# A two-layer residual kernel: the second product of odd units cut in two around the first, and low-rank banks copied out by the scalar engine

## The chip, the cores and the metric

The kernel runs on one core of a Trainium2 chip. TensorE (PE) multiplies, VectorE (DVE) adds and subtracts, ScalarE (ACT) copies, GpSimd (POOL) and SyncE (SP) issue transfers. The metric is device time in microseconds, the median of three runs; a profile of one execution shows where it goes.

## The reference

All data are fp32. `x` has 32 sequences of 128 rows and 2048 columns. Two layers are added one after the other:

```python
x = x + (einsum('bsi,oi->bso', x, W0) + bias
         + scale[id0][:, None, None] * einsum('bsr,bor->bso', einsum('bsi,bri->bsr', x, A[id0]), B[id0]))
x = x + einsum('bij,bkj->bik', x, W1[id1])      # W1: 16 matrices of 2048x2048, one chosen per sequence
```

`W0` is one 2048x2048 matrix for all sequences. `A` and `B` are low-rank adapters of rank 16, chosen per sequence.

## The kernel before, in words

**Two stages.** Stage one computes the first layer for all sequences, stage two the second layer, pair of sequences by pair of sequences. Both replace multiplications by sums: a block product is done with seven products in place of eight. In stage one this is done twice over: seven *phases* (`PHASES`) on the outside, and in each of them seven products P1 to P7 inside a unit. `PHASES[i]` says which blocks of `x` (A terms) and of `W0` (W terms) DVE has to add up, which partial result the unit reads and writes, and whether it finishes a quarter of the output (`final`).

**Units.** Stage one is a list of 56 units: 7 phases x 2 groups of sequences x 4 column blocks, in that order, so a group change comes every four units. Phases 3 to 6 (units 24 to 55) are final. Of these, units 24 to 31 also write a new partial result; the code calls them `apart`. In units 32 to 55 the even ones are `late` and the odd ones `ahead`.

**Accumulators.** The eight PSUM banks are pairs a, b and c (one of each for even and for odd units) and the two banks d and l. A product of four matmuls (`product`, L500) puts 128x512 results into one bank. The order in a unit, on PE, is P1 into a; P2 into b; P6 onto a; P5 into c; P7 onto a; P3 onto c; P4 onto a. So P6 can't start before ACT has copied P1's result out of bank a into `p1` (L619). ACT likewise copies `u2` (L648) after P6, `p5` (L651) after P5, `u3` (L656) after P7, and the last quarter (L687) after P4. DVE adds the pairs b+p1, c+u2 and u3+p5 into quarters of the result `z`.

**The low-rank part.** `add_low` (L511) multiplies the low-rank factors of a unit, four short matmuls for each of four banks. In an `apart` unit it runs at the unit's start, into b, c, d and l; DVE then adds each of the four banks to a tile of `x` (`low_to_x`), and the products reuse b and c. In a `late` (even) unit it runs at the unit's end, for the unit itself onto b, c, a and into d, and for the odd unit that follows into that unit's b, c, a and bank l. Of the odd unit's four, b stays where it is, and P2 is accumulated onto it, which is why P2 comes before P1 there:

```python
            if ahead:
                product(2, b, n, False)
            if n != 1:
                product(1, a, n, True)
                nc.scalar.copy(p1, a)
                if not ahead:
                    product(2, b, n, True)
```

The other three banks (a1, c1 and l in the code) are read out by DVE in `low_to_x`, the first of them ahead of three adds of the even unit's own quarters.

**What sets the order.** The order of instructions on every engine is the order of the text; nothing is scheduled by a planner. An engine waits at an instruction until the semaphores that the framework derived from its operands are reached. `finish(n-1)`, called at the start of unit n, adds partial results and `x` to `z` and stores it by POOL. `w_terms`, `w_sums`, `a_terms` and `a_sums` are the DVE sums for units and groups to come. Loads are begun by `Loads.pump` on SP's queue, in a fixed list, as soon as a slot of `mem` is free; slots are freed as DVE and PE finish with them. `evp` holds one buffer for each of p1, u2, p5 and u3.

**Unit 0** also does P1 and P2 of unit 1, and keeps the copy of P1 in a tile of its own, `p1_next`.

**Stage two** (L728) has 7168 recorded matmuls of 128x512 into the same eight banks, on weights that SP loads two steps ahead.

Of the kernel before, what the change touches and what calls it, by code (L numbers as in the profile page):

```python
# [9 lines left out]
F32 = mybir.dt.float32  # L10
# [62 lines left out]
def cond_resid_kernel(  # L73
# [56 lines left out]
    nc = tc.nc  # L130
    B, S, D = out.shape
    NW, _, _, _, P, _, _, NF = w1q.shape
# [44 lines left out]
    def add(dst, a, b):  # L177
        nc.vector.tensor_tensor(dst, a, b, ALU.add)  # L178
# [83 lines left out]
    with tc.tile_pool(name="c0", bufs=1) as c0, tc.tile_pool(  # L262
        name="ev", bufs=1
# [17 lines left out]
        def view(slot, *shape):  # L281
            names = "abcd"[: len(shape)]
            return mem[:, slot].rearrange(
                f"p ({' '.join(names)}) -> p {' '.join(names)}", **dict(zip(names[1:], shape[1:]))
            )
# [39 lines left out]
        def early(n):  # L325

            return n < len(units) and PHASES[units[n][0]][4] and (
                PHASES[units[n][0]][3] or n % 2 == 1
            )
# [58 lines left out]
        def make_scale():  # L388

            id0_f = c0.tile([P, B // 4], F32, tag="id0f", name="id0_f")  # L390
            nc.vector.tensor_scalar(id0_f, id0r_sb, 0.0, float(NA - 1), ALU.max, ALU.min)
            hit = c0.tile([P, B // 4], F32, tag="hit", name="hit")
            for n in range(NA):
                nc.vector.tensor_scalar(
                    hit if n else scale, id0_f, float(n), scl[:, n : n + 1],
                    ALU.is_equal, ALU.mult,
                )
                if n:
                    add(scale, scale, hit)
# [85 lines left out]
        def load_b(n):  # L485
            i, g, o = units[n]
            r, c, _ = PHASES[i][4]
            b_sel = bsp.tile([P, 4, P], F32, tag="b_sel", name="b_sel")
            for t in range(2):
                for s in range(4):  # L490
                    m = adapter(id0_ok, 16 * r + 8 * g + 4 * t + s, NA - 1, POOL)
                    nc.gpsimd.dma_start(  # L492
                        out=b_sel[ts(t, 2 * RT), s],
                        in_=bt[ds(m, 1), c, o].rearrange("o j r m -> (o j r) m"),
                    )
            return b_sel

        def product(k, dst, n, start):
            for i in range(4):
                nc.tensor.matmul(  # L500
                    dst, lhsT=wts[n][k][:, i, :], rhs=acts[n // 4][k][:, i, :],
                    start=(start and i == 0), stop=(i == 3), skip_group_check=True,
                )

        def add_low(n, dsts, starts):

            i, g, o = units[n]
            r = PHASES[i][4][0]
            for s in range(4):
                for q, (dst, start) in enumerate(zip(dsts, starts)):  # L510
                    nc.tensor.matmul(  # L511
                        dst[:, ts(s, S)], lhsT=b_sels[n][ts(q, RT), s], rhs=low[r, g][ts(q, RT), s],
                        start=(start and s == 0), stop=(s == 3), skip_group_check=True,
                    )
# [2 lines left out]

            return z.rearrange("p (t s j m) -> p t s j m", t=2, s=4, j=2)[:, t, :, j]

        def low_to_x(n, q, src):  # L520
            xs = view(loads.slot(("x", n)), 4, NF)[:, q]
            add(xs, src, xs)

# [57 lines left out]
        for n, (i, g, o) in enumerate(units):  # L581
            _, _, old, new, final = PHASES[i]
            a, b, c = (x[n % 2] for x in (bank_a, bank_b, bank_c))
            z = mem[:, 19 + n % 2]
            group = n // 4
            more = group + 1 < 2 * len(PHASES)
            lowering = more and (group + 1) // 2 == LOW
            apart = bool(new and final)
            late = final and not early(n)
            ahead = early(n) and not apart  # L590
            p1, u2, p5, u3 = (
                evp.tile([P, NF], F32, tag=k, name=k) for k in ("p1", "u2", "p5", "u3")
            )
            if n == 1:
                p1 = p1_next
            if n + 1 < len(units) and PHASES[units[n + 1][0]][4]:
                b_sels[n + 1] = load_b(n + 1)
            if apart:
                low_banks = b, c, bank_d, bank_l
                add_low(n, low_banks, (True,) * 4)  # L600
                for q in range(4):
                    low_to_x(n, q, low_banks[q])
            if n:
                finish(n - 1)
            if n == 2:
                make_scale()
            if n == len(units) - 2:
                load_w1(0)
            if 0 < n < len(units) - 1:
                wts[n + 1] = w_sums(n + 1)  # L610
            elif n:
                second_loads()
            sums = a_sums(group + 1) if more and o == 3 else iter(())

            if ahead:
                product(2, b, n, False)
            if n != 1:
                product(1, a, n, True)
                nc.scalar.copy(p1, a)  # L619
                if not ahead:  # L620
                    product(2, b, n, True)
            if n == 0:
                p1_next = c0.tile([P, NF], F32, tag="p1_next", name="p1_next")
                product(1, bank_a[1], 1, True)
                nc.scalar.copy(p1_next, bank_a[1])
                product(2, bank_b[1], 1, True)
            if lowering:
                lowrank(group + 1, o)
                loads.done(("a", group + 1, o))
            if more:  # L630
                a_terms(group + 1, o)
            if n + 2 < len(units):
                w_terms(n + 2)
            if lowering and o % 2 == 1:
                lowrank_out(group + 1, o // 2)
            ends = n + 1 == len(units)
            if ends:
                rest = mem[:, loads.slot(("U4", n))]
                for t in range(2):
                    dst = rest.rearrange("p (t s j m) -> p t j s m", t=2, s=4, j=2)[:, t]  # L640
                    add(dst, dst, view(loads.slot(("x", n)), 2, 2, 4, S)[:, t])
                loads.done(("x", n))
            if not late:
                add(zq(z, 0, 0), by_seq(b), by_seq(p1))
            if ends:
                add(zq(z, 0, 0), zq(z, 0, 0), zq(rest, 0, 0))
            product(6, a, n, False)
            nc.scalar.copy(u2, a)  # L648
            next(sums, None)
            product(5, c, n, True)  # L650
            nc.scalar.copy(p5, c)  # L651
            if ends:
                fourth = sums_w1(0)
            next(sums, None)
            product(7, a, n, False)
            nc.scalar.copy(u3, a)  # L656
            add(zq(z, 1, 1), by_seq(u3), by_seq(p5))
            if ends:
                add(zq(z, 1, 1), zq(z, 1, 1), zq(rest, 1, 1))
                sums_x1(0, 0)  # L660
            next(sums, None)
            product(3, c, n, False)
            if not late:
                add(zq(z, 0, 1), by_seq(c), by_seq(u2))
            if ends:
                add(zq(z, 0, 1), zq(z, 0, 1), zq(rest, 0, 1))
                store_x1(n, 0)
            product(4, a, n, False)
            next(sums, None)
            if late:  # L670
                add_low(n, (b, c, a, bank_d), (False, False, False, True))

                b1, c1, a1 = (x[1 - n % 2] for x in (bank_b, bank_c, bank_a))
                add_low(n + 1, (b1, c1, a1, bank_l), (True,) * 4)
                low_to_x(n + 1, 2, a1)
                add(zq(z, 0, 0), by_seq(b), by_seq(p1))
                add(zq(z, 0, 1), by_seq(c), by_seq(u2))
                add(zq(z, 1, 1), by_seq(bank_d), zq(z, 1, 1))
                low_to_x(n + 1, 1, c1)
                low_to_x(n + 1, 3, bank_l)  # L680
            if ends:
                add(zq(z, 1, 0), by_seq(a), zq(rest, 1, 0))
                store_x1(n, 1)
                loads.done(("U4", n))
                fourth()
            else:
                nc.scalar.copy(zq(z, 1, 0), by_seq(a))  # L687
            loads.done(("W", n, 0))
            if o == 3:
                for q in range(4):  # L690
                    loads.done(("A", group, q, 0))


    with tc.tile_pool(name="c1", bufs=1) as c1:
# [6 lines left out]
        for n in range(last + 1):  # L701
# [22 lines left out]
            for k in (1, 6, 7, 5, 2, 3, 4) if n == last else (1, 7, 2, 3, 5, 6, 4):  # L724
                dst = bank[:, banks[k]]
# [108 lines left out]
```

## Time and profile before

| | |
|---|---|
| median of three runs | 2988.7 us (2988.65 to 2988.78) |
| the profiled execution | 2988.26 us, span 2986.6 us |
| PE busy | 2964.9 us (99%) |
| DVE busy | 2351.8 us (79%) |
| ACT busy | 183.6 us (6%) |
| POOL busy | 239.0 us (8%) |
| mean transfer rate | 343 GB/s |
| stage one ends | about 1443.5 us |

The span is the time from the first to the last instruction of the profile; the execution's own time is 1.66 us more. In the profile's rows "p" stands for p1 and p5, "u" for u2 and u3, since buffer numbers are left out, and "mem", "bank" and "tset" are the big tiles. L178 and L181 are the one-line helpers `add` and `sub` through which all DVE adds and subtractions go, so their rows hold many uses. One fp32 matmul of the code leaves two records, and two weight loads. The time behind a row in square brackets is that for which the engine stood idle before it, and what ended that.

### The profile page before, as it was taken

Reading aid. Unit: us, or ns where it says so; the run is one execution under the profiler, and the core shown is the slowest. Engines: PE = TensorE matmul, PEld = TensorE weight load, DVE = VectorE, ACT = ScalarE, POOL = GpSimd, SP = SyncE. Lnnn points to the kernel's source line nnn. Section 1 sums busy time; section 2 is a strip of 40 time slices with the busy share of each in tenths; the row PEclk is TensorE's granted clock in tenths of the full one; section 3 lists DMA queues with packets and bytes.
Section 4 is the critical chain, followed back from the end, with each engine's and each line's share of the span. In section 5 each row is a group of like instructions: output and inputs, shape, how many; then the busy total and the mean of one; then the engine's idle time right before and its main releaser. Section 6 shows DMA issues by size and latency. Waiting matters only on the chain.

```text
span 2986.6 us, 32858 instructions
## 1 busy us (share of the span) xinstructions
PE 2964.9 (99%) x12384; PEld 1171.9 (39%) x12384; DVE 2351.8 (79%) x1717; ACT 183.6 (6%) x312; POOL 239.0 (8%) x427
## 2 busy tenths in 40 slices
PE   9999999999999999999999999999999999999999
PEld 4445444444444444444333333333333333333333
DVE  3467755467645768873999999999999999999997
ACT  1111111111111111111000000000000000000000
POOL 1111000022212222221000000000000000000000
PEclk9999999999999999999999999999999999999999
DMA  5679866789865889986899999999999999999995
GB/s 225 257 307 368 322 258 268 270 302 345 323 259 208 312 340 374 380 319 261 335 399 392 387 387 410 385 400 386 405 387 398 386 388 405 392 395 386 403 391 220
DMA packets 186014, 1025.61 MB, mean 343 GB/s; under 512 B 23808, under 2 KB 23808, under 8 KB 79616
## 3 DMA queue, kind: packets, MB, share of 16 engines
q1 hardware_dynamic: 142512, 906.68, 76.7%
q0 software_dynamic: 25248, 83.92, 7.4%
q10 hardware_dynamic: 18096, 32.91, 3.5%
q8 instruction: 98, 1.61, 0.2%
q14 instruction: 60, 0.49, 0.0%
HBM read 922.76 MB, written 100.66 MB: 343 GB/s over the span
## 4 chain that ended last, share of the span: by engine, by line
PE 74%; DVE 1%; DMA 0%; ACT 0%; issue 0%; ACTq 0%; DVEq 0%
PE bank L728 52%; PE bank L500 22%; PE bank L511 1%; DMA mem<-in_w0q_dram 0%; DVE mem L178 0%; ACT p L619 0%; DVE mem L181 0%; DVE tset L181 0%; DVE res L178 0%; ACTq L619 0%; DVEq L178 0%; DVEq L181 0%
## 5 line engine op out<-in xcount | busy, mean ns | idle before, releaser
L181 DVE TENSOR_TENSOR mem<-mem 128x2048 f32<-128x2048 f32 (+1 forms) x733 | 1483.1, 2052 | 42.5 <-DMA mem<-in_w0q_dram 16.0
L728 PE MATMUL bank<-mem 128*64 128x512 f32 x5120 | 1120.6, 592 | 0.0
L500 PE MATMUL bank<-mem 128*128 128x512 f32 x1792 | 792.7, 595 | 6.2 <-DVE mem L178 4.7
L728 PEld LDWEIGHTS bank<-mem 128*64 128x64 f32 x5120 | 367.7, 137 | 731.1 <-issue 695.2
L500 PE MATMUL bank<-mem,tset 128*128 128x512 f32 x1344 | 597.1, 594 | 9.2 <-ACT p L619 9.2
L500 PEld LDWEIGHTS bank<-mem 128*128 128x128 f32 x1792 | 339.6, 191 | 429.5 <-issue 421.4
L728 PE MATMUL bank<-mem,s 128*64 128x512 f32 x2048 | 461.2, 592 | 0.0
L178 DVE TENSOR_TENSOR mem<-mem 128x2048 f32<-128x2048 f32 (+2 forms) x195 | 338.8, 1750 | 101.8 <-ACT mem L687 51.4
L500 PEld LDWEIGHTS bank<-mem,tset 128*128 128x128 f32 x1344 | 253.5, 190 | 333.3 <-issue 309.2
L728 PEld LDWEIGHTS bank<-mem,s 128*64 128x64 f32 x2048 | 147.1, 137 | 292.4 <-issue 291.5
L178 DVE TENSOR_TENSOR mem<-u,p 128x512 f32<-128x512 f32 x56 | 38.7, 691 | 213.8 <-ACT u L656 213.8
L492 POOL DMA_DIRECT2D b_sel<-in_bt_dram x256 | 134.7, 526 | 349.7 <-PE bank L511 186.5
L178 DVE TENSOR_TENSOR mem<-bank,mem 128x512 f32<-128x512 f32 x81 | 51.4, 684 | 104.4 <-PE bank L511 104.4
L734 ACT COPY pv<-bank 128x512 f32<-128x512 f32 x32 | 18.8, 586 | 1516.1 <-PE bank L728 1136.2
L178 DVE TENSOR_TENSOR pv<-bank,pv 128x512 f32<-128x512 f32 x64 | 44.3, 692 | 78.4 <-PE bank L728 77.4
L181 DVE TENSOR_TENSOR tset<-mem,tset 128x512 f32<-128x512 f32 x112 | 77.2, 689 | 7.9 <-PE bank L500 4.1
L178 DVE TENSOR_TENSOR mem<-bank,u 128x512 f32<-128x512 f32 x56 | 38.5, 688 | 53.8 <-PE bank L500 53.8
L178 DVE TENSOR_TENSOR mem<-mem,ident 128x1024 f32<-128x1024 f32 x64 | 78.1, 1220 | 0.0
L530 POOL DMA_DIRECT2D x1t<-mem x64 | 49.0, 770 | 224.3 <-DVE mem L178 220.4
L648 ACT COPY u<-bank 128x512 f32<-128x512 f32 x56 | 32.8, 586 | 356.9 <-PE bank L500 353.1
L687 ACT COPY mem<-bank 128x512 f32<-128x512 f32 x55 | 32.2, 586 | 356.2 <-PE bank L500 242.9
L619 ACT COPY p<-bank 128x512 f32<-128x512 f32 x55 | 32.2, 586 | 231.1 <-PE bank L500 224.8
(40 smaller groups left out, 507.9 us busy)
## 6 DMA issues: line engine op xcount, KB each, us to landing
mem<-in_w1q_dram SPq DMA_DIRECT2D x512, 1024.0 KB, 10.2
mem<-in_xq_dram SPq DMA_DIRECT2D x119, 1024.0 KB, 12.6
mem<-in_w0q_dram SPq DMA_DIRECT2D x111, 1024.0 KB, 6.8
mem<-U SPq DMA_DIRECT2D x40, 1024.0 KB, 9.4
mem<-in_xq_dram SPq DMA_DIRECT2D x66, 512.0 KB, 7.9
x1t<-mem POOLq DMA_DIRECT2D x64, 512.0 KB, 8.9
mem<-x1t SPq DMA_DIRECT2D x64, 512.0 KB, 10.0
out_dram<-res ACTq DMA_DIRECT2D x124, 256.0 KB, 6.1
```

The costliest lines, as they stand in the source:

```text
L178: nc.vector.tensor_tensor(dst, a, b, ALU.add)
L181: nc.vector.tensor_tensor(dst, a, b, ALU.subtract)
L492: nc.gpsimd.dma_start(out=b_sel[ts(t, 2 * RT), s], in_=bt[ds(m, 1), c, o].rearrange("o j r m -> (o j r) m"),)
L500: nc.tensor.matmul(dst, lhsT=wts[n][k][:, i, :], rhs=acts[n // 4][k][:, i, :], start=(start and i == 0), stop=(i == 3), skip_group_check=True,
L511: nc.tensor.matmul(dst[:, ts(s, S)], lhsT=b_sels[n][ts(q, RT), s], rhs=low[r, g][ts(q, RT), s], start=(start and s == 0), stop=(s == 3), s ...
L530: nc.gpsimd.dma_start(out=x1t[4 * r + 2 * g + t][:, :, 8 * c + 2 * o : 8 * c + 2 * o + 2].rearrange("s p j m -> p s (j m)"), in_=view(19 + ...
L619: nc.scalar.copy(p1, a)
L648: nc.scalar.copy(u2, a)
L687: nc.scalar.copy(zq(z, 1, 0), by_seq(a))
L728: nc.tensor.matmul(dst[ts(j, M)], lhsT=xts[pair, k4 // 2][k][:, j, k4 % 2 * 2 + i], rhs=w1s[n][k][:, j, i], start=(k4 == 0 and i == 0), st ...
L734: nc.scalar.copy(pv[:, 0], dst)
```

## The change

`product` takes the list of its matmuls as an argument. In `ahead` units only the first two matmuls of P2 come before P1, and the other two come after P1 and its copy. A tile `kept` of two banks' size is added; `p1_next` becomes its first half. `low_to_x` can have ACT copy the bank into `kept` first, and DVE then adds from `kept`: this is done for banks b and c of the `apart` units (q = 0 and 1) and for bank a1 of the odd unit in `late` units, where the copy comes in ACT's order ahead of the copy of the last quarter (L687). DVE's adds and their order stay, as do the number and order of all loads and stores.

```diff
-        def product(k, dst, n, start):
-            for i in range(4):
+        def product(k, dst, n, start, some=range(4)):
+            for i in some:
...
+        kept = c0.tile([P, 2, NF], F32, tag="kept", name="kept")
+
-        def low_to_x(n, q, src):
+        def low_to_x(n, q, src, k=None):
+            if k is not None:
+                nc.scalar.copy(kept[:, k], src)
+                src = kept[:, k]
             xs = view(loads.slot(("x", n)), 4, NF)[:, q]
             add(xs, src, xs)
...
                 for q in range(4):
-                    low_to_x(n, q, low_banks[q])
+                    low_to_x(n, q, low_banks[q], q if q < 2 else None)
...
             if ahead:
-                product(2, b, n, False)
+                product(2, b, n, False, (0, 1))
             if n != 1:
                 product(1, a, n, True)
                 nc.scalar.copy(p1, a)
-                if not ahead:
-                    product(2, b, n, True)
+                product(2, b, n, not ahead, (2, 3) if ahead else range(4))
             if n == 0:
-                p1_next = c0.tile([P, NF], F32, tag="p1_next", name="p1_next")
+                p1_next = kept[:, 0]
...
-                low_to_x(n + 1, 2, a1)
+                low_to_x(n + 1, 2, a1, 0)
```

## The prediction

> **What bounds the kernel now.** I read the busy table first (PE 2964.9 of 2986.6 us), then what TensorE waited for, then the chain of waits in order of time, then the timelines of PE, DVE and ACT at each gap found. Busy PE is not PE at its peak, so I count weight loads: inside a product they stand 0.43 us apart (6.86 us for 16 records, 0.4288 each). A written matmul leaves two records, so a product of four is 8 records, 3.43 us.
>
> What TensorE waited for (us in total, times, longest):
>
> ```profile
> PE bank L500 <- ACT p L619: 9.2, 13, 0.7
> PE bank L500 <- DVE mem L178: 4.7, 1, 4.7
> PE bank L500 <- DMA mem<-in_xq_dram: 1.5, 1, 1.5
> ```
>
> Beyond these (and 1.5 us at the start) PE is gap-free; stage two (L728, from 1443.5 us) has no gap at all. So the kernel is PE's program plus these waits, and only they can be won. The chain shows the first kind, once per pair of units from unit 33 on:
>
> ```profile
> 853.75 7.08 PE bank L500 x16
> 860.90 0.59 ACT p L619
> 861.49 0.04 issue
> 861.54 41.47 PE bank L500 x96
> ```
>
> The 16 records are P2 and P1 of an odd unit. P6 follows at once into P1's bank, so it waits for ACT's copy of that bank. The marked idle is 0.72 us, but the loss is larger. The last P1 weight load is at 1270.66 in the pair I followed; an unbroken stream has P6's third load at 1270.66+3x0.4288 = 1271.94, and it came at 1272.93: **0.99 us**. The chain agrees: these pairs repeat every 51.25 us; 112 records in one stretch (48.26, units 31 and 32) and the low-rank products (2.00) make 50.26.
>
> The second kind is one place, unit 28. PE's timeline, then DVE's:
>
> ```profile
> 719.48 3.70 PE L500 MATMUL bank<-mem 128*128 128x512 f32 x8
> 727.87 6.68 PE L500 MATMUL bank<-mem 128*128 128x512 f32 x8 [4.69 <-DVE mem L178]
> 734.39 7.03 PE L500 MATMUL bank<-mem,tset 128*128 128x512 f32 x16
> ```
>
> ```profile
> 724.93 2.28 DVE L181 TENSOR_TENSOR mem<-mem 128x2048 f32<-128x2048 f32 x1
> 727.13 2.48 DVE L178 TENSOR_TENSOR mem<-bank,mem 128x512 f32<-128x512 f32 x4
> ```
>
> P1 ran at 719.48; P2 needs bank b, which the first of four DVE adds must read out, and DVE had older work until 727.13. P2 then took 6.52 us to the next product instead of 3.43. The stretches table tells why (busy of PE, weight load, DVE, ACT, POOL; then PE's clock, DMA share, GB/s):
>
> ```profile
> 727.80:731.00 3.20, 3.13 (x4) 1.50 (x5) 3.20 (x5) 0.00 (x0) 0.00 (x0) 0.50 0.25 105
> ```
>
> Clock 0.50. From P1's start here to the next unit's is 752.75-719.48 = 33.27 us; a gap-free unit of this kind takes 25.34 (752.82 to 778.16). The place costs **7.93 us**.
>
> [...] 0.50 after 4.69 us, 1.00 after 0.72. [...] Here the copy is 586 and the add 684 from a bank, 686 from SBUF, so an add that changes source costs the same.
>
> **The change part by part.**
>
> (a) *ACT copies b and c in the eight units 24 to 31.* 16 copies x 0.586 = 9.4 us of ACT, which is 6% busy. In unit 28 ACT's L687 copy ran 718.48 to 719.07; the low-rank products end at about 719.5, so b is out by about 720.1 and c by 720.8. P2 is due at 722.9, P5 about 10 us after P1's start. The DVE adds keep number and length and read `kept`. Next late there would be P6 (s2, DVE done 721.6, due 726.4), P7 (724.4 against 733) and P3 (727.2 against 737): none waits. Banks d and l are read by 729.6, wanted by unit 29 about 744. In units 29 to 31 DVE was waiting for PE (3.83 us before 752.84); DMA share is 0.84 from 727.8 to 828, so 16 us of transfer time are free to follow PE. Gain 7.93. The other seven units had no gap: 0.
>
> (b) *P2 split 2+2 round P1 in the 12 odd units 33 to 55.* No instruction added. P6's first load is now five pitches, 2.14 us, behind P1's last; the wait needs 1272.39-1270.66 = 1.73. The copy is covered by 0.41 us. Gain 12 x 0.99 = 11.9.
>
> (c) *The price of the split: P1 follows half of P2.* P1 writes bank a1, where unit n+1's low-rank part lies. ACT's new copy (12 x 0.586 = 7.0 us in all) can start when DVE's read did, 1264.69, 0.15 after P2 begins at 1264.54, and frees the bank at about 1265.32; P1 is due 4 records on, 1266.25. Cover 0.93 us. ACT was idle 7.37 us there. The copy of quarter z10 (L687), now queued behind, ran at 1263.79 and would end near 1265.9; its reader (`finish`, 1268.28) has 2.4 us.
>
> (d) *DVE's chain in those units starts 0.6 us later*, since its first add awaits ACT's copy; five adds queue behind, the last but one freeing c1, by about 1268.9, for P5 at about 1274.8. Hidden. Loads come from DVE's releases, SP's order is unchanged, and POOL's only new wait is one store's on ACT. b is now finished after P1, but its z00 add runs at 1282: nothing.
>
> (e) *Given back at unit 46.* PE stood 0.61 us at 1193.93 because P1's copy into `p1` waited for unit 45's z00 add:
>
> ```profile
> 1183.80 2.29 DVE L181 TENSOR_TENSOR mem<-mem 128x2048 f32<-128x2048 f32 x1 [4.82 <-DMA mem<-in_w0q_dram]
> ...
> 1192.52 0.68 DVE L178 TENSOR_TENSOR mem<-bank,p 128x512 f32<-128x512 f32 x1
> ```
>
> DVE had waited only 1.35 us for PE since unit 43 (1110.07 to 1161.32) and then waits for a transfer at DMA share 1.02. PE will come 1.98 us earlier (units 43 and 45), DVE not: the wait grows to about 2.6 us. Unknown: if all loads move with PE, nothing is lost[...]. I take 2.0 from 0 to 5. After it DVE has 4.32 us to spare (1213.44) and 7.54 (1264.69).
>
> (f) *Start of stage two.* DVE is busy without a break from 1418 to 1449. s3 is done about 1441.7, later by 0.6; the second product wants it at 1445.2, now 1444.2. 1.9 us remain. Stage two then moves whole.
>
> Sum: 7.93+11.9-2.0 = **17.8 us**. The profiled execution took 2988.26 (span 2986.6 and 1.66 round it), 0.44 under the median 2988.7 of three runs; from the median, 2970.9.
>
> **The rivals.**
>
> *B, transfers set the pace.* From 1109.6 to 1263.2 the DMA share is 0.99. If that holds PE to its old pace through units 37 to 51, 8 x 0.99 of the gain goes: 17.8+2.0-7.9 = 11.9, 2976.8. For: the share. Against: SP's waits there are mostly for slots, and DVE waits on PE again at 1161, 1213 and 1264.
>
> *C, slower: ACT's copy of a1 becomes the wait ahead of P1.* Place: 12 odd units. It decides when a1 is free more than 0.93 us after my estimate; every us beyond costs 12. Break-even is 0.93+17.8/12 = 2.4 us late; 3 us late gives 12x2.07-17.8 = 7 us slower, 2996. For: the copy is a new link. Against: nothing but PE releases it, and ACT is idle.
>
> *D, unit 28 stays.* ACT frees b but another DVE result holds PE there: 11.9-2.0 = 9.9, 2978.8. Against: due times in (a).
>
> *E, the split does nothing* because the copy's 0.41 us cover is not there, and D in part: under 6 us, no difference.
>
> **How the numbers follow.** 0.2% is 6.0 us, about what a measurement of this kernel can tell from no change. A 0.68, B 0.18, D 0.06, C 0.04, E 0.04. Faster is A, B and D, 0.92; within 0.04; slower 0.04. A alone spans 2968 (nothing lost at unit 46) to 2974 (5 lost). The range adds B, with a little beyond it, 2967.5 to 2978.
>
> **What would show it.** Right: the DVE wait of 4.7 us gone and PE's clock 1.00 near 728 us; ACT p waits from 13 to about one, near unit 46, some 2 to 3 us long; `kept` copies of 586 ns, 28 of them; pairs of 50.3 us. Wrong: a new PE wait on ACT's copy ahead of P1 (C), PE waits for DVE or transfers between 1000 and 1260 us (B), a half-clock stretch left near 720 (D), or gaps in stage two.

## The result, and the profile after

The changed kernel takes 2974.26 us (median of six runs, 2972.55 to 2975.17) against 2988.74 for the kernel before (six runs, 2988.02 to 2992.57): 14.5 us less, a ratio of 0.9948 with a 95% interval of 0.9936 to 0.9961. In microseconds that interval is 11.7 to 19.1. The profiled execution took 2974.56 us, its span 2972.9. It is faster, though 3.4 us short of the forecast of 2970.9, and inside its range.

What TensorE waited for after (us in total, times, longest):

```profile
PE bank L500 <- DMA mem<-in_xq_dram: 3.1, 1, 3.1
PE bank L500 <- ACT p L624: 2.5, 1, 2.5
```

Both aims are met. The wait for DVE at unit 28 is gone, and of 13 waits for ACT's copy of P1 one is left. (L624 is what was L619, L691 what was L687, L732 what was L728.) But the wait for the first transfers has doubled, from 1.5 to 3.1 us, and the one wait on ACT has grown from 0.6 to 2.5.

The chain of waits after: start, length, what.

```profile
998.77 2.00 PE bank L511 x64
1000.77 48.26 PE bank L500 x112
1049.03 2.00 PE bank L511 x64
```

A pair of units is now one unbroken piece of 112 records between two low-rank blocks, and repeats every 50.26 us in place of 51.25. Unit 28, on PE, ACT and DVE:

```profile
723.65 7.13 PE L500 MATMUL bank<-mem 128*128 128x512 f32 x16
730.62 7.03 PE L500 MATMUL bank<-mem,tset 128*128 128x512 f32 x16
```

```profile
723.74 1.07 ACT L524 COPY kept<-bank 128x512 f32<-128x512 f32 x2 [0.50 <-PE bank L511]
```

```profile
729.68 2.28 DVE L181 TENSOR_TENSOR mem<-mem 128x2048 f32<-128x2048 f32 x1
731.88 1.29 DVE L178 TENSOR_TENSOR mem<-kept,mem 128x512 f32<-128x512 f32 x2
```

DVE is as late as before (its add comes 8.2 us after P1's start, 731.88-723.65; it was 7.65, 727.13-719.48). Nobody on PE waits for it: ACT had emptied both banks 1.2 us after P1's start, and P1 and P2 are one piece of 16. There is no idle stretch of PE, and the granted clock is 1.00 throughout (stretch table, last three columns: granted clock, DMA share, GB/s):

```profile
724.00:824.00 100.00, 100.00 (x321) 45.33 (x320) 76.07 (x71) 15.16 (x28) 25.16 (x44) 1.00 0.90 343
```

And unit 46, where the forecast gave something back, on PE and on DVE:

```profile
1185.18 7.13 PE L500 MATMUL bank<-mem,tset 128*128 128x512 f32 x16 [2.54 <-ACT p L624]
```

```profile
1175.49 2.29 DVE L181 TENSOR_TENSOR mem<-mem 128x2048 f32<-128x2048 f32 x1 [5.02 <-DMA mem<-in_w0q_dram]
...
1183.77 0.68 DVE L178 TENSOR_TENSOR mem<-bank,p 128x512 f32<-128x512 f32 x1
```

It is the same chain as before (a transfer, DVE's sums, unit 45's z00 add, ACT's copy into `p1`, P6), with PE waiting longer at its end.

**Two marks divide the kernel for what follows.** From unit 28's low-rank products to the first matmul of stage two, the profile before has 1443.50-718.37 = 725.13 us, the profile after 1429.81-722.55 = 707.26: **17.9 less**, where the sum had 17.8. Up to the first mark, where the change touches next to nothing, after is 4.2 us *later*, and PE's timeline shows that it is so from the first 30 microseconds on: behind the wait of 3.06 us the clock was 0.50 from 16 to 20 us, and 24 records took 13.45 us for 10.54 before. So the shortfall in this pair of profiles lies there, and the experiments ask what it is, and whether the 17.9 repeats.

### The profile page after: what moved, and what is told of

It is laid out like the page before. It is cut to its first block, busy times and chain, and to the rows that moved or that the text cites. A ratio compares the mean times of both kernels' runs of the same rounds, so it can differ in the third digit from the quotient of the medians.

```text
span 2972.9 us, 32939 instructions
## 1 busy us (share of the span) xinstructions
PE 2961.1 (100%) x12384; PEld 1174.1 (39%) x12384; DVE 2351.3 (79%) x1717; ACT 197.7 (7%) x340; POOL 239.1 (8%) x427
## 4 chain that ended last, share of the span: by engine, by line
PE 98%; DMA 1%; DVE 1%; issue 0%; SPq 0%; ACT 0%; DVEq 0%; ACTq 0%
PE bank L732 52%; PE bank L500 44%; PE bank L511 1%; PE bank L467 1%; DMA mem<-in_w0q_dram 0%; DMA mem<-in_xq_dram 0%; DVE mem L178 0%; DVE mem L181 0%; DVE tset L181 0%; SPq L303 0%; SPq L298 0%; DVE res L178 0%; ACT p L624 0%; ACT kept L524 0%; DVEq L178 0%
## 5 line engine op out<-in xcount | busy, mean ns | idle before, releaser
L732 PE MATMUL bank<-mem 128*64 128x512 f32 x5120 | 1120.7, 592 | 0.0
L732 PEld LDWEIGHTS bank<-mem 128*64 128x64 f32 x5120 | 367.9, 137 | 730.9 <-issue 692.7
L732 PE MATMUL bank<-mem,s 128*64 128x512 f32 x2048 | 461.2, 592 | 0.0
L732 PEld LDWEIGHTS bank<-mem,s 128*64 128x64 f32 x2048 | 147.2, 137 | 292.3 <-issue 292.3
L178 DVE TENSOR_TENSOR mem<-kept,mem 128x512 f32<-128x512 f32 x28 | 18.7, 690 | 106.4 <-ACT kept L524 106.4
L691 ACT COPY mem<-bank 128x512 f32<-128x512 f32 x55 | 32.3, 587 | 267.8 <-PE bank L500 255.3
L178 DVE TENSOR_TENSOR mem<-bank,p 128x512 f32<-128x512 f32 x55 | 37.7, 685 | 10.0 <-PE bank L500 6.2
## 6 DMA issues: line engine op xcount, KB each, us to landing
mem<-in_xq_dram SPq DMA_DIRECT2D x119, 1024.0 KB, 12.9
```

What stands on the lines that cost most here:

```text
L732: nc.tensor.matmul(dst[ts(j, M)], lhsT=xts[pair, k4 // 2][k][:, j, k4 % 2 * 2 + i], rhs=w1s[n][k][:, j, i], start=(k4 == 0 and i == 0), st ...
```

## The experiments

**The changed kernel again.** Theory: the start is chance. Rival: the change brought it.

> The changed kernel once more. Its profile began stage one's unit 28 at 723.7 us, 4.2 us later than the profile before did, although nothing that runs there was changed. Theory S (chance at the start: the first transfers land at another moment in each execution[...]): the runs scatter over some 3 us between 2971 and 2975, and this profile shows the start either with a wait near 1.5 us at full clock or near 3 us at half clock. Rival R2 (the change itself costs 4 us at the start): every run stays near 2974.3 and this profile shows the wait of about 3 us and clock 0.50 between 12 and 20 us again.

Measured 2974.03 (2970.37 to 2977.02), a scatter of 6.7 us. Its first wait was 2.7 us, at full clock, and the first mark stood at 718.85, 0.5 from before. But the stretch between the marks was 1428.80-718.85 = 709.95, 2.7 longer than in the other profile of the same kernel. On PE, and in the stretch table (granted clock third from the end):

```profile
1182.47 8.83 PE L500 MATMUL bank<-mem,tset 128*128 128x512 f32 x16 [3.52 <-ACT p L624]
```

```profile
1184.00:1188.00 4.00, 4.00 (x8) 1.67 (x7) 3.97 (x4) 0.05 (x1) 0.04 (x1) 0.70 1.00 416
```

The wait at unit 46 was 3.52 us, and the 16 records after it took 8.83 in place of 7.13, part of them at half clock (a mean of 0.70 in those 4 us). Only the edge of my range had room for that (5 us lost at unit 46, an estimate); it happens.

**Only ACT's copies of b and c.**

```diff
-                product(2, b, n, False, (0, 1))
+                product(2, b, n, False)
...
-                product(2, b, n, not ahead, (2, 3) if ahead else range(4))
+                if not ahead:
+                    product(2, b, n, True)
...
-                low_to_x(n + 1, 2, a1, 0)
+                low_to_x(n + 1, 2, a1)
```

> Of the change only ACT's copies of banks b and c in units 24 to 31; P2 stays whole ahead of P1 and DVE reads a1. Theory: only unit 28 gains, 7.9 us, so 2980.8 if the start is as in the profile before, up to 4.2 more (2985) if it is as in the profile after; the 12 ACT p waits of 0.72 us stay, PE's DVE wait of 4.7 us goes, clock 1.00 near unit 28. Unit 46's wait stays near 0.6 us. Rival D (another DVE result holds PE in unit 28): a PE wait on DVE remains there and the gain is under 5.

Measured 2980.53 (2979.57 to 2981.9), ratio 0.9974 (0.9963 to 0.9984); against 2988.38 for before on the same chip 7.85 us, forecast 7.93 (the interval of the ratio is 4.8 to 11.1 us). Its waits, then PE in unit 28 and at the start of unit 29:

```profile
PE bank L500 <- ACT p L624: 8.6, 12, 0.7
```

```profile
721.40 7.13 PE L500 MATMUL bank<-mem 128*128 128x512 f32 x16
746.73 7.13 PE L500 MATMUL bank<-mem 128*128 128x512 f32 x16
```

There are twelve waits of 0.72 us and none for DVE. Unit 28 takes 746.73-721.40 = 25.33 us for 33.27 before, so the place gave back 7.94. A miss: the short wait at unit 46 went too, where I expected it to stay. Counted from the first mark, the product before P6 there began 7.9 us earlier than before (1180.27-720.30 for 1186.29-718.37), but DVE's z00 add 8.8 us earlier (1185.66-720.30 for 1192.52-718.37). So the stretch between the marks, 1436.63-720.30 = 716.33, is 8.8 shorter than before: unit 28, and what unit 46 had lost.

**Only P2 in two parts**, DVE reading a1:

```diff
-                    low_to_x(n, q, low_banks[q], q if q < 2 else None)
+                    low_to_x(n, q, low_banks[q])
...
-                low_to_x(n + 1, 2, a1, 0)
+                low_to_x(n + 1, 2, a1)
```

> Of the change only P2 in two parts round P1; no ACT copies, DVE reads a1 as before. Theory: DVE's read of a1 (1264.69 to 1265.37 in the profile before) ends 0.9 us ahead of P1's new due time, so the split needs no copy: 12 x 0.99 - 2.0 = 9.9 us, 2978.8 (2983 with the later start), no PE wait on DVE ahead of P1, unit 28 still at 7.9 lost. Rival R1 (the split lives on ACT's copy of a1): P1 waits for DVE in several of the 12 units, and the gain is well under 9.

Measured 2979.49 (2977.79 to 2981.96), ratio 0.9968 (0.9957 to 0.9979): 8.9 us (6.3 to 12.9), where 9.9 was forecast. Pairs take 50.26 us, there is no wait ahead of P1, and unit 28's loss is still there:

```profile
731.41 5.29 PE L500 MATMUL bank<-mem 128*128 128x512 f32 x8 [5.79 <-DVE mem L178]
1190.83 8.83 PE L500 MATMUL bank<-mem,tset 128*128 128x512 f32 x16 [2.27 <-ACT p L624]
```

At unit 46 there was half clock behind a wait of 2.27 us (a mean of 0.57 from 1192 to 1196 us), shorter than the 2.54 that left the clock alone in the profile after.

**No copy of a1**: the changed kernel with the last edit above alone.

> The changed kernel without ACT's copy of a1: DVE reads it, as before. Theory: the copy is worth nothing, since DVE's read ends 0.9 us ahead of P1 (and in unit 45, where DVE comes late, still in time by some 0.3 us): 2974, no PE wait on DVE ahead of P1. Rival R1: P1 waits for DVE in units where DVE is late; a wait of about 1 us in one or two of the twelve, 2975 to 2976.

Measured 2973.13 (2971.84 to 2974.43). The copy of a1 is worth nothing that can be measured, as theory said. Its tightest place is unit 45, on DVE and PE:

```profile
1152.16 0.69 DVE L178 TENSOR_TENSOR mem<-bank,mem 128x512 f32<-128x512 f32 x1 [0.36 <-PE bank L511]
```

```profile
1152.01 7.13 PE L500 MATMUL bank<-mem 128*128 128x512 f32 x16
```

Even there DVE stood ready and waited 0.36 us for PE, and the first half of P2, P1 and the second half of P2 stay one piece.

**P2 cut 3+1**, to test the cover of ACT's copy of P1.

```diff
-                product(2, b, n, False, (0, 1))
+                product(2, b, n, False, (0, 1, 2))
...
-                product(2, b, n, not ahead, (2, 3) if ahead else range(4))
+                product(2, b, n, not ahead, (3,) if ahead else range(4))
```

> The changed kernel with P2 cut 3+1 round P1 in place of 2+2. Theory (the split hides the copy of p1, with 0.41 us to spare at 2+2): P6's first weight load is due 3 pitches, 1.29 us, behind P1's last, and the wait needs 1.73, so each of the 12 odd units loses 0.44 us: 12 ACT p waits come back, and the time is 12 x 0.44 = 5.3 us longer, less up to 1 us that unit 46's wait then shrinks by: 2978 to 2979.5. Rival (the clock and the start make the difference, the copy is hidden by any work behind P1): no ACT p waits but the one at unit 46, and 2974.

Measured 2973.62 (2971.79 to 2977.22), not 5 us slower. This is a miss. The number is the rival's, but not for the rival's reason, since ACT's copy is not hidden any more. Weight loads at one place:

```profile
1259.94 0.19 PEld L500 LDWEIGHTS bank<-mem 128*128 128x128 f32 x1 [0.24 <-issue]
...
1261.67 0.30 PEld L500 LDWEIGHTS bank<-mem,tset 128*128 128x128 f32 x2 [0.69 <-ACT p L624]
1262.21 0.19 PEld L500 LDWEIGHTS bank<-mem,tset 128*128 128x128 f32 x1 [0.24 <-issue]
```

P6's load waits for ACT. It comes 1.73 us behind P1's last (1259.94), as I had worked out, and 0.44 after its due time (1259.94+3x0.4288 = 1261.23). But the two loads then take 0.30 us together, and the third comes at 1262.21 where an unbroken stream has 1259.94+5x0.4288 = 1262.08. So a lateness of 0.44 us cost 0.13 here. Pairs repeat every 50.39 us (844.83 to 895.22), 12x0.13 = 1.6 us in all, which the scatter hides.

**A second buffer for P1's copy in even late units**, in the half of `kept` that is free once unit 31 is done.

```diff
             if n == 1:
                 p1 = p1_next
+            elif late:
+                p1 = kept[:, 1]
```

> The changed kernel with P1's copy of even late units going into the second half of kept in place of p1, so that in unit 46 it needn't wait for unit 45's z00 add. Theory: the wait of 2.5 to 3.5 us there is a write behind a late read of one buffer; it goes, and with it the half-clock stretch behind it in those executions that had one: 2.5 to 5 us, median 2969.5 to 2971.5, no PE wait after 20 us. Rival B (transfers set the pace there): PE is held a product or two later by another result of DVE (u2 or the next sums) for about as long, and the time stays at 2974.

Measured **2969.32** (2967.68 to 2970.32), ratio to before 0.9937 (0.9924 to 0.9951). After the start there is no wait of PE at all. ACT's copy, P6 and DVE's z00 add of unit 45 at unit 46:

```profile
1175.16 0.59 ACT L626 COPY kept<-bank 128x512 f32<-128x512 f32 x1 [2.85 <-PE bank L500]
```

```profile
1178.40 7.03 PE L500 MATMUL bank<-mem,tset 128*128 128x512 f32 x16
```

```profile
1180.00 0.68 DVE L178 TENSOR_TENSOR mem<-bank,p 128x512 f32<-128x512 f32 x1
```

ACT copied at 1175.16, 4.8 us before DVE's z00 add (1180.00) began to read the old buffer. The stretch between the marks is 1422.93-718.46 = 704.47 us; the changed kernel has 2.79 more in one profile and 5.48 in the other. So the wait was the single buffer, and the transfers behind DVE held up nothing else: rival B falls.

**Five matmuls of the identity in unit 0's wait** (their result is not used), in three kernels.

```diff
                 product(1, a, n, True)
                 nc.scalar.copy(p1, a)
+                if n == 0:
+                    for _ in range(5):
+                        nc.tensor.matmul(bank_l[:, :P], lhsT=ident, rhs=ident, start=True, stop=True)
```

In the changed kernel:

> The changed kernel with five more 128x128 matmuls of the identity into bank l between P1 and P2 of unit 0, about 2 us of PE work inside the wait for the first transfers; their result is not used. Theory S and R2 both say that PE's idle time there falls under 2 us and the clock stays at 1.00, which saves the half-clock stretch (about 2.6 us) in those executions that have it. S: median 2971 to 2973 and a narrower scatter; R2: every run 2.6 us faster, near 2971.7. If the clock halves all the same, 2974 and the half-clock stretch is still in the profile.

2972.99 (2970.87 to 2974.3). With the second buffer:

> Both: the five identity matmuls in unit 0's wait, and the second buffer for p1. Theory: no idle stretch of PE over 1.5 us is left, so the clock stays at 1.00 throughout, the scatter of the runs is that of the first transfers alone (about 1.5 us), and the median is 2969 to 2970. Rival: as the better of the two alone, 2970 to 2973, with the same scatter of 4 us or more.

**2968.71** (2967.62 to 2970.64), ratio 0.9935 (0.9922 to 0.9949); again 704.47 us between the marks. In the kernel before:

> The kernel before with the five identity matmuls in unit 0's wait (their result is not used). S: it gains what the changed kernel gained from them, about 1 us, 2987.3, within the noise. R2: the start before was at full clock anyway and the filler gains nothing or costs up to 0.5 us, 2988.4 to 2989.

2988.25 (2986.72 to 2989.54), ratio 0.9999 (0.9991 to 1.0007). In all three profiles the clock at the start was 1.00 (first waits 0.7, 1.5 and 1.1 us), but no median moved by more than 1.1 us and the scatter stayed near 3 us. The filler is worth nothing that these runs can tell; I had expected more. That it holds the clock up isn't shown either: of the ten profiles without it, five have the clock at 1.00 there too, behind first waits of up to 3.19 us. The five took 1.28 us, not the 2 that I had estimated.

**The kernel before, twice more**, for its start.

> The kernel before, a second profile, for its start and unit 28. Theory S (the start is chance): PE's wait in unit 0 is anywhere from 1.5 to 3.5 us, as in the eight profiles of changed kernels so far (1.9 to 3.5), with or without a half-clock stretch. R2 (the start became slower with the change): a wait near 1.5 us at full clock again.

> A third profile of the kernel before, for the same question: S says a wait in unit 0 anywhere from 1.5 to 3.5 us, R2 says near 1.5 us again. Unit 28's wait for DVE should be 4 to 6 us with half clock behind it, unit 46's near 0.6 us at full clock, in both.

They took 2990.47 and 2990.14 us, one run each. The first waits were 2.7 and 2.6 us. Unit 28's wait for DVE was 6.6 and 4.9 us, the first of them above what I expected. In the third profile part of the time after the first wait is at half clock (means of 0.77 and 0.81 in the two windows of 4 us from 12 us on):

```profile
14.13 12.23 PE L500 MATMUL bank<-mem 128*128 128x512 f32 x24 [2.61 <-DMA mem<-in_xq_dram]
```

24 records took 12.23 us here, 10.54 in the profile before. So a first wait of 2.6 us and more, and a start partly at half clock, come without the change too. The rival, that the change brings the late start, finds no support in them; the 1.5 us of that first profile was a short wait.

## Why the prediction was right, and where it was off

**(a), banks b and c: right.** 7.93 was forecast; unit 28 gave back 7.94 in the profile with that half alone. (That its medians give 7.85 is in part chance, since unit 46's wait went too.) The loss was an idle stretch and the slow clock behind it, and reading the length of P2's group (6.52 for 3.43) as part of the place's cost made the difference between 4.7 and 7.9. In the profile before, PE was busy in unit 28 from 727.87 on, and its clock was 0.50 in each microsecond from 728 to 733, 0.54 in the next, and then 1.00: slow for about 6 us. The forecast took the place's length as measured.

**(b), the split: right.** Pairs take 50.26 us with the 2+2 split. The stretches of the two kernels in which unit 46 lost nothing, banks alone and two buffers, differ by 716.33-704.47 = 11.86 us; 11.9 was forecast. One term in it was mis-sized: the cover. I counted 0.41 us to spare from one weight load to the next; the 3+1 cut shows that a load 0.44 us behind its due time costs only 0.13.

**(c), P1 behind half of P2: right, for a weaker reason.** ACT's copy began 0.15 us after P2 (1254.95 and 1254.80 in the pair I checked). P1 never waited. But it wouldn't have waited for DVE either. Rival C never came near its point.

**(d) and (f): right.** There was no wait on DVE ahead of P5, and no gap in stage two.

**(e), unit 46: the mechanism was right, the size off.** I took 2.0 us more than before. The loss there, against the 704.47 of the two kernels with two buffers, was 2.79 us in the first profile after: the 2.0, and 0.78 that were lost there before (P6 at 1193.93, due 16 records after 1186.29, at 1193.15). It was 5.48 in the second, and 6.45 (710.92) in the filled kernel, since half clock followed the wait. The 5 us that I allowed at most were an estimate. Half clock followed waits of 3.52, 3.29, 2.77 (the 3+1 cut) and 2.27 us (P2 alone), and not those of 2.54 and 1.87 (no copy of a1), so the length of the wait alone didn't tell whether it would come. The cost of half clock belonged into the middle of the sum, not at its edge. (A slip besides: with nothing lost at unit 46 the sum gives 2988.7-19.8 = 2968.9, not 2968.)

**Rivals B, D and E** fell with these readings: from 1100 to 1253 us, at a DMA share of 0.99, PE waits at unit 46 alone (B); PE waits for nothing in unit 28 (D); and the split works (E).

**Where the 3.4 us are.** Part of them is unit 46. By the medians the single buffer cost 4.7 us (2974.03 to 2969.32), or 3.8 against the kernel without the copy of a1 (2973.13), which was timed on the same chip. The sum had 2.0 and the 0.78 of before, so this term makes 1.0 to 1.9 us of the shortfall.

The start is the other candidate, and it was missing from the sum. The sum was made against one profile, in which PE waited 1.5 us for its first data. That was the shortest of all profiles without filler; the others had 1.9 to 3.5. In the first pair of profiles the start is the whole of the shortfall. For the medians this isn't shown. The forecast started from the median before, from which that profile was only 0.44 us away; and with the three profiles of the kernel before and the two of the changed one, the means to the first mark are 719.5 and 720.7, 1.2 apart, where two profiles of the changed kernel differ by 3.7. What unit 46 doesn't explain is 1.5 to 2.4 us; that is within the scatter of single executions (up to 6.7 us) and stays open.

## What to carry to other kernels

A wait that follows from one buffer being read late can be taken away by an engine with nothing to do that empties it early, as by ACT here (6% busy, both banks out 1.2 us after P1's start); but ask of each copy whether the late reader is late *there* (for banks b and c it was, for a1 not). When PE gets faster, look for the place where the producer behind a transfer sets the pace, and give that place its second buffer in the same change: it was worth a third as much again as the change itself, 4.7 us (2974.03 to 2969.32). And before a forecast to a few microseconds, take a second profile of the same kernel and divide both at marks: the start and the clock differ from one execution to the next (in the three of the kernel before, first waits of 1.5, 2.7 and 2.6 us, the last of them with half clock behind it).

## What the runs showed of the hardware

In these profiles PE's clock didn't halve at a fixed length of waiting. In the kernel before it was 1.00 after 0.72 us (from 1272.4 us on) and 0.50 after 4.69 (unit 28). In unit 0 it stayed at 1.00 after 3.19 us (the 3+1 cut) and 2.73 (the changed kernel again), and fell to 0.67 and 0.90 in the 4 us windows after 1.94 us (banks alone). At unit 46 it fell to 0.57 after 2.27 us (P2 alone) and stayed at 1.00 after 2.54 (the profile after). What it cost when it fell came in two sizes: about 1.7 us (8.83 for 7.13, and 12.23 for 10.54), or 2.6 to 3.1 us (in unit 28, 6.02 for 3.43 in the filled kernel before and 6.52 for 3.43 in the profile before; 10.03 for 7.13, behind 3.29 us in the filled changed kernel; 13.45 for 10.54, behind 3.06 us in the profile after). No profile shows a cost between them.

In the two places that I followed, a weight load that came late delayed what followed by less than its lateness: 1.30 us late cost 0.99 in the kernel before, and 0.44 late cost 0.13 with the 3+1 cut. The stream of loads took up 0.31 us both times; two loads after the wait took 0.30 us together, where two steps in the stream were 0.86.
